# A graph layer's edge kernel: bias row, silu order, column counts and tail rearranged

## The chip, the cores and the metric

The kernel runs on one core of one Trainium2 chip. The metric is device time in microseconds (us) of one execution. TensorE is PE, VectorE DVE, ScalarE ACT, GpSimd POOL and SyncE SP. Each engine works off its own instruction stream in order; DMAs are issued by SP, ACT and POOL.

## The reference

12,500 nodes with 64 numbers each, 400,000 edges sorted by destination, 16 numbers per edge:

```python
m_in = jnp.concatenate([x[src], x[dst], edge_attr], axis=-1)
h = jax.nn.silu(m_in @ W1 + b1)
messages = jax.nn.silu(h @ W2 + b2)
agg = jax.ops.segment_sum(messages, dst, num_segments=x.shape[0])
out = layernorm(x + silu(concatenate([x, agg]) @ W3 + b3))
```

W1 is 144 x 64, W2 64 x 64, W3 128 x 64; all is float32.

## The kernel before, in words

128 edges are a tile, 3125 in all; 8 tiles are an octet (391), and three octets a chunk (131) whose dst and edge attributes are loaded together (`load`, L427 to L436: two `dr` DMAs and one `oh` DMA on SP). As the edges are sorted by dst, the destinations of an octet lie in a window of 48 nodes.

The first layer is a sum of three parts in PSUM (`first_layer`, L457). x[src] W1 comes ready from a table `pa` in HBM, gathered by POOL with one indirect DMA for each tile (`gather`, L396), and transposed by PE (L476). x[dst] W1 and the edge attributes come out of one product (L480): its weights `xw` hold the window's rows times W1 (`window_product`, L420, then `window_copy`, L425) and the attribute rows of W1, its data `oh` the one-hot of dst (`compare_dst`, L447) and the attributes. ACT applies silu with the bias `b1s` (L483). Two octets later PE does the second layer (`second_layer`, L492 and L494) and ACT its silu (L498); four octets later PE sums the messages by node with a second one-hot `eh` (L453; `add_up`, L507), and six later DVE adds the sums to `agg` (`add_window`, L512).

POOL is relieved in two ways. For some octets the first two tiles (a "pair") aren't gathered: ACT and DVE copy x[src] column by column, 64 partitions by 4 bytes, out of `xs`, a copy of x in SBUF, at addresses that they read into registers (`columns`, L294 to L303). ACOLS and VCOLS say how many columns each engine copies per octet and how they are cut into parts, LOADS how many addresses are read at once. PE multiplies the pair by W1 (`w1d`, L479). The indices of a pair come by a small DMA on SP (`index`, L374, tile `cxi`, three buffers), and DVE turns them into addresses (`address`, L382). For every 16th octet the second two tiles (`rx`) are fetched by SP, 16 rows of 256 bytes per octet (`rows`, L343 for the 16 addresses, L347 for the 16 DMAs).

The loop over octets (L626) writes out the order of PE, ACT, DVE and SP by hand; POOL's order is left to the framework. In one round o, SP issues the indices of pairs that begin in round o + 3, the chunk's load two octets ahead (L655), the window's x three octets ahead (`window_load`, L415, three buffers), and last the 16 rows. POOL gathers three octets ahead into five buffers. ACT: 32 columns, silu of octet o, 28 columns, silu of the second layer of octet o - 2. DVE: `agg`, `oh` of octet o + 1, 32 columns, `xw` and `eh` of octet o + 1, 32 columns.

When all edges of a group of 512 nodes (25 groups) are summed, its node layer is done between octets: `node_load`, `node_product` (L539 to L542, nine products), `node_silu` (L548), `node_stats`, and later, by batches of five groups, the root (L562), `divide` (L572) and `store` (L577). They are hung on rounds by `later`. The last two groups come after the loop, with a check of whether the windows held (L700 to L716); if not, a slow general form runs, which it doesn't here.

Of the kernel before, what the change touches and what calls it, by code (L numbers as in the profile page):

```python
# [20 lines left out]
P = 128  # L21
# [12 lines left out]
ACOLS = (32, 28)  # L34
VCOLS = (32, 32)
ROWS = 16
LOADS = (16, 8)
XBASE = (0, 64 << 18)
XADDR = 36864
# [61 lines left out]
def windows(ctx, tc, ident, badi, pa, x, xt, src_c, src_row, dst_c, dst_row, attr_t, dst_2, attr_2, base, w1, b1, w2, b2, w3, b3, out, edges):  # L101
# [33 lines left out]
    b1s = const.tile([P, 1], F32, name="b1s")  # L135
# [3 lines left out]
    for s in range(2):  # L139
        h = slice(s * D, (s + 1) * D)  # L140
        nc.scalar.dma_start(w1d[h, h], w1[0:D, :])
        nc.scalar.dma_start(b1s[h, :], b1.rearrange("(k o) -> k o", o=1))
# [93 lines left out]
    w1bb = fast.tile([D, 2, D], F32, name="w1bb")  # L236
    nc.vector.tensor_copy(w1bb, w1ab[:, 1:2, :].to_broadcast([D, 2, D]))
# [13 lines left out]
    with tc.tile_pool(name="gat", bufs=AHEAD + 2) as gat, tc.tile_pool(name="drp", bufs=2) as drp, \  # L251
# [3 lines left out]
            tc.tile_pool(name="msg", bufs=THIRD - SECOND + 1) as msg, tc.tile_pool(name="win", bufs=3) as win, \  # L255
# [3 lines left out]
            tc.tile_pool(name="cx", bufs=4) as cx, tc.tile_pool(name="cxi", bufs=3) as cxi, \  # L259
# [46 lines left out]

        def begun(o):

            first, behind = -(-(o - RAW) * RATE // (2 * P)), -(-(o + 1 - RAW) * RATE // (2 * P))
            return range(max(0, first), max(0, min(behind, len(pairs))))  # L310

        def index(o):
            for j in begun(o):
                t = cxi.tile([1, 2 * P], I32, name="cxi")
                e = octs[pairs[j]][1] * P
                nc.sync.dma_start(t, src_row[:, e:e + 2 * P])
                indices[j] = t

        def address(o):
            for j in begun(o):  # L320
                t = indices[j]
                for s in range(2):
                    h = slice(s * P, (s + 1) * P)
                    nc.vector.tensor_scalar(t[:, h], t[:, h], 4.0, float(XBASE[s] + XADDR), op0=OP.mult, op1=OP.add)

# [84 lines left out]
        def window_load(o):  # L410
            if o % 4 == 0:
                bases(ENG.SP, o)
            xr = win.tile([D, 2, S], F32, name="xr")
            frm = xt[:, ds(winreg.pop((ENG.SP, o)), S)]
            nc.sync.dma_start(xr, frm[:, None, :].to_broadcast([D, 2, S]))  # L415
            winrow[o] = xr
# [7 lines left out]
        def window_copy(o):  # L424
            nc.vector.tensor_tensor(xw[o % 3][:E, :], winrow.pop(o)[:E, :], mask[:E, :], op=OP.mult)  # L425
# [31 lines left out]
        def first_layer(o):  # L457
# [25 lines left out]
            nc.scalar.activation(h[:, :k], p1[:, :k], AF.Silu, bias=b1s)  # L483
# [48 lines left out]
        def node_product(q):  # L532
            c, n = groups[q]
            p = n // G
            assert p * G == n
            po = mis.tile([P, G, D], F32, name="mm")
            av = agg[:, c:c + n].rearrange("k (p i) -> k i p", i=G)
            xv = xs[0:D, c:c + n].rearrange("k (p i) -> k i p", i=G)
            nc.tensor.matmul(po[:p], ones[:, :p], b3r, start=True, stop=False, skip_group_check=True)  # L539
            for i in range(G):  # L540
                nc.tensor.matmul(po[:p, i, :], xv[:, i], w3x, start=False, stop=False, skip_group_check=True)  # L541
                nc.tensor.matmul(po[:p, i, :], av[:, i], w3s, start=False, stop=(i == G - 1), skip_group_check=True)  # L542
            nodes[q].append(po)
# [41 lines left out]
        todo = {}  # L585

        def later(o, f, *a):
            todo.setdefault(min(o, NO), []).append((f, a))
# [4 lines left out]
        for q in range(early):  # L593
            o = lead[due[q]] + LAST - 1 if q < rest else NO
            later(o - 1, node_load, q)
            later(o, node_product, q)
            later(o, node_silu, q)
            later(o + 2, node_stats, q)
        for q0, q1 in batches:
            o = lead[due[q1 - 1]] + LAST - 1  # L600
            later(o + 3, root, q0, q1)
            later(o + 4, inverse, q0, q1)
            for r in range(q1 - q0):
                later(o + 4 + 2 * r, divide, q0 + r)
                later(o + 5 + 2 * r, store, q0 + r)

# [16 lines left out]
        with tc.manual_schedule(engines={ENG.PE, ENG.Activation, ENG.DVE, ENG.SP}):  # L623
            compare_dst(0)
            compare_nodes(0)
            for o in range(NO + THIRD):  # L626
# [28 lines left out]
                if o + 2 < NO and octs[o + 2][3] and o + 2:  # L655
                    load(octs[o + 2][0])
# [38 lines left out]
                if o < NO:  # L695
                    for f, a in todo.get(o, []):
                        f(*a)


        evi = xs.bitcast(I32)[:, :3 * NCH]  # L700
        nc.gpsimd.iota(evi, pattern=[[STEP, NCH], [0, 3]], base=0, channel_multiplier=0)
        lag = xs[:, 3 * NCH:3 * NCH + NO]
        nc.vector.tensor_tensor(lag, evi[:, :NO], wb, op=OP.subtract)
        lim = nv.tile([P, 3], F32, name="lim")
        nc.vector.tensor_reduce(lim[:, 0:1], lims[:, 0, :], AX.X, OP.min)
        nc.vector.tensor_reduce(lim[:, 1:2], lims[:, 1, :], AX.X, OP.max)
        nc.vector.tensor_reduce(lim[:, 2:3], lag, AX.X, OP.max)
        bad = nv.tile([P, 3], F32, name="bad")
        nc.vector.tensor_scalar(bad[:, 0:1], lim[:, 0:1], 0.0, None, op0=OP.is_lt)
        nc.vector.tensor_scalar(bad[:, 1:2], lim[:, 1:2], float(S - 1), None, op0=OP.is_gt)  # L710
        nc.vector.tensor_scalar(bad[:, 2:3], lim[:, 2:3], float(LAG), None, op0=OP.is_gt)
        pc = mis.tile([1, 3], F32, name="mm")
        nc.tensor.matmul(pc, onec, bad, start=True, stop=True)
        bs = nv.tile([1, 1], F32, name="bs")
        nc.vector.tensor_reduce(bs, pc, AX.X, OP.add)
        nc.vector.tensor_copy(badi, bs)  # L716

        for o in range(NO + THIRD - LAST, NO):
            add_window(o)
        for f, a in todo.get(NO, []):  # L720
# [268 lines left out]
```

## Time and profile before

| | us |
|---|---|
| median of 3 runs (3440.99 to 3442.54) | 3441.17 |
| the profiled execution | 3453.06 |
| its span, first to last instruction | 3450.7 |
| POOL's last gather starts | 3399.90 |
| ACT's last first-layer silu starts | 3424.22 |
| mean granted TensorE clock | 0.68 |

The page of the profile gives busy time by engine and groups of instructions by line (L396 is line 396). A group's row reads: line, engine, operation, tile written <- tiles read, shapes, count | busy time, mean ns of one | idle time of the engine just before it, and who ended most of it. "issue" is idle time in which the engine waited for nothing that the profile shows. A source view lists one line's instructions with the least, median and longest duration and the first and last start. SPq, ACTq and POOLq are the engines' instruction sequencers.

### The profile page before, as it was taken

Reading aid. Unit: us, or ns where it says so; the run is one execution under the profiler, and the core shown is the slowest. Engines: PE = TensorE matmul, PEld = TensorE weight load, DVE = VectorE, ACT = ScalarE, POOL = GpSimd, SP = SyncE. Lnnn points to the kernel's source line nnn. Section 1 sums busy time; section 2 is a strip of 40 time slices with the busy share of each in tenths; the row PEclk is TensorE's granted clock in tenths of the full one; section 3 lists DMA queues with packets and bytes.
Section 4 is the critical chain, followed back from the end, with each engine's and each line's share of the span. In section 5 each row is a group of like instructions: output and inputs, shape, how many; then the busy total and the mean of one; then the engine's idle time right before and its main releaser. Section 6 shows DMA issues by size and latency. Waiting matters only on the chain. (4 is left out here: it accounts for less than half of the span.)

```text
span 3450.7 us, 104586 instructions
## 1 busy us (share of the span) xinstructions
PE 2554.8 (74%) x13750; PEld 1649.2 (48%) x13750; DVE 2517.4 (73%) x26396; ACT 2717.7 (79%) x23405; POOL 2569.0 (74%) x2724
## 2 busy tenths in 40 slices
PE   6877777777777677776777777777777677677777
PEld 4444544444445445444444445444445454444454
DVE  2477777777777777777777777777777777777775
ACT  2388788788887887888878888887788777878886
POOL 7777777777777777777777777777777777777773
PEclk9666667666667666776666666666666666766767
DMA  7423323323332332333332332333323323333322
GB/s 159 95 53 68 63 59 65 65 61 60 77 61 61 68 62 60 65 65 65 64 69 59 62 68 61 62 75 61 62 60 69 60 61 66 69 62 62 67 61 52
DMA packets 203931, 229.79 MB, mean 67 GB/s; under 512 B 133612, under 2 KB 141988, under 8 KB 202324
## 3 DMA queue, kind: packets, MB, share of 16 engines
q1 hardware_dynamic: 101528, 122.61, 16.1%
q0 software_dynamic: 86880, 89.14, 14.1%
q10 hardware_dynamic: 14812, 11.26, 1.4%
q14 instruction: 595, 4.87, 0.5%
q8 instruction: 116, 1.90, 0.2%
HBM read 216.36 MB, written 6.40 MB: 65 GB/s over the span
## 5 line engine op out<-in xcount | busy, mean ns | idle before, releaser
L396 POOL DMA_INDIRECT ga<-pa,sc x2619 | 2475.4, 945 | 802.2 <-issue 711.9
L303 ACT COPY cx<-xs 64x4 uint8 x22560 | 2216.5, 188 | 166.8 <-issue 122.0
L301 DVE TENSOR_REDUCE cx<-xs 64x4 uint8 x24032 | 1782.6, 150 | 544.7 <-issue 477.8
L507 PEld LDWEIGHTS pg<-eh,m 128*64 128x64 f32 x6250 | 301.0, 182 | 1046.8 <-issue 331.1
L507 PE MATMUL pg<-eh,m 128*64 128x48 f32 x6250 | 351.3, 271 | 580.9 <-DVE agg L512 523.0
L480 PE MATMUL p<-oh,xw 128*128 128x512 f32 (+1 forms) x758 | 601.0, 887 | 132.3 <-DVE xw L425 130.0
L494 PE MATMUL p<-w2d,h 128*128 128x128 f32 x3126 | 674.8, 383 | 0.0
L494 PEld LDWEIGHTS p<-w2d,h 128*128 128x128 f32 x3126 | 573.8, 275 | 133.1 <-issue 133.1
L498 ACT ACTIVATE m<-p 128x512 f32<-128x512 f32 x391 | 232.2, 594 | 255.5 <-PE p L494 249.0
L447 DVE TENSOR_TENSOR oh<-dr,wrow 96x512 f32<-96x512 int32 x391 | 264.4, 676 | 209.1 <-DMA dr<-in_dst 121.6
L483 ACT ACTIVATE h<-p,b1s 128x512 f32<-128x512 f32 x391 | 267.3, 684 | 139.2 <-PE p L480 86.1
L476 PE MATMUL p<-ident,ga 128*128 128x128 f32 x1310 | 336.9, 389 | 41.4 <-DMA ga<-pa,sc 41.4
L420 PE MATMUL mm<-w1bb,xr 64*96 64x128 f32 x782 | 252.9, 418 | 62.0 <-DMA xr<-in_xt 36.7
L476 PEld LDWEIGHTS p<-ident,ga 128*128 128x128 f32 x1310 | 199.6, 190 | 133.3 <-issue 110.3
L480 PEld LDWEIGHTS p<-oh,xw 128*128 128x128 f32 x758 | 176.7, 287 | 169.3 <-DVE xw L425 168.8
L453 DVE TENSOR_TENSOR eh<-wrow,dc 128x384 f32<-128x384 f32 x391 | 211.7, 541 | 0.0
L420 PEld LDWEIGHTS mm<-w1bb,xr 64*96 64x96 f32 x782 | 134.2, 224 | 140.2 <-issue 61.4
L492 PE MATMUL p<-b2r,one 3*128 3x512 bf16 x391 | 196.4, 502 | 0.0
L512 DVE TENSOR_TENSOR agg<-agg,pg 128x48 f32 x391 | 78.1, 200 | 74.2 <-PE pg L507 40.0
L479 PE MATMUL p<-cx,w1d 128*128 128x128 f32 x364 | 105.2, 387 | 22.7 <-ACT cx L303 22.7
L425 DVE TENSOR_TENSOR xw<-mm,mask 96x128 f32<-96x128 f32 x391 | 109.4, 280 | 13.4 <-PE mm L420 7.6
L396 POOL DMA_INDIRECT ga<-in_x,sc x96 | 91.5, 953 | 30.2 <-issue 27.7
(83 smaller groups left out, 767.6 us busy)
## 6 DMA issues: line engine op xcount, KB each, us to landing
rx<-pa SPq DMA_DIRECT2D x5888, 0.2 KB
dr<-in_dst SPq DMA_DIRECT2D x260, 288.0 KB
ga<-pa,sc POOLq DMA_INDIRECT x2619
oh<-in_attr SPq DMA_DIRECT2D x130, 192.0 KB
xr<-in_xt SPq DMA_DIRECT2D x391, 24.0 KB
xs<-in_xt ACTq DMA_DIRECT2D x12, 512.0 KB
pa<-v ACTq DMA_DIRECT2D x12, 256.0 KB
xa<-in_x SPq DMA_DIRECT2D x24, 128.0 KB
```

The costliest lines, as they stand in the source:

```text
L301: nc.vector.tensor_reduce(to, frm[:, :, None], AX.X, OP.max)
L303: nc.scalar.copy(to, frm)
L396: nc.gpsimd.indirect_dma_start(out=ga[:, i, :], out_offset=None, in_=x if o < RAW else pa[:, :], in_offset=bass.IndirectOffsetOnAxis(ap=sc ...
L420: nc.tensor.matmul(pw[:E, :], winrow[o].rearrange("k s w -> k (s w)"), w1bb.rearrange("k s m -> k (s m)"), start=True, stop=True)
L447: nc.vector.tensor_tensor(oh[:E, :], dr[:, e:e + w], wn[:E, o:o + 1].to_broadcast([E, w]), op=OP.is_equal)
L453: nc.vector.tensor_tensor(eh[:, :n], row[:, None, :].to_broadcast([P, n, S]), rel[:, t0:t0 + n, None].to_broadcast([P, n, S]), op=OP.is_equal)
L476: nc.tensor.matmul(p1[:, i, :], g2.rearrange("p s d -> p (s d)"), ident, is_transpose=True, start=(i == c), stop=False, skip_group_check=True)
L480: nc.tensor.matmul(p1[:, :k], xw[o % 3], oh, start=False, stop=True, skip_group_check=True)
L483: nc.scalar.activation(h[:, :k], p1[:, :k], AF.Silu, bias=b1s)
L494: nc.tensor.matmul(p2[:, 2 * i:2 * i + 2, :].rearrange("p s d -> p (s d)"), h[:, i, :], w2d, start=False, stop=(i == k - 1), skip_group_ch ...
L498: nc.scalar.activation(m[:, :n2], p2[:, :n2], AF.Silu)
L507: nc.tensor.matmul(pg[s * D:(s + 1) * D, :], m[:, i, :], eh[:, i, :], start=(i < 2), stop=(i >= n - 2), skip_group_check=True)
```

## The change

- b1 leaves the silu. The window product gets a 65th row: `w1bb` holds b1 there, and three fixed tiles `xr0` to `xr2` hold ones (they replace the pool `win`).
- `node_silu` of round o is done after the first-layer silu of round o + 1 (`behind`).
- A chunk's dst and attributes are loaded three octets ahead instead of two.
- ACT copies 40 + 32 columns per octet for 32 + 28; DVE copies 64 as before, in four parts of 16 around `xw` and `eh`. Addresses are read by 16. There are 196 pairs for 182; a pair is used one octet later, `cx` has five buffers for four, and pairs stop six octets from the end.
- XADDR, the address of `xs`, follows its new place.
- The end: the check `limits` and its product move into the last rounds (its iota on POOL stands ahead of the last 13 gathers), the last two groups load their x at round NO - 2, and their b3 and x products are done in round NO + 1, ahead of the last two sums.

```diff
-ACOLS = (32, 28)
-VCOLS = (32, 32)
+ACOLS = (40, 32)
+VCOLS = (16, 16, 16, 16)
-LOADS = (16, 8)
+LOADS = (16, 16)
-XADDR = 36864
+XADDR = 36832
+QUIET = 6
...
-    w1bb = fast.tile([D, 2, D], F32, name="w1bb")
-    nc.vector.tensor_copy(w1bb, w1ab[:, 1:2, :].to_broadcast([D, 2, D]))
+    w1bb = fast.tile([D + 1, 2, D], F32, name="w1bb")
+    nc.vector.tensor_copy(w1bb[:D], w1ab[:, 1:2, :].to_broadcast([D, 2, D]))
+    nc.sync.dma_start(w1bb[D:, :, :], b1.rearrange("(o s k) -> o s k", o=1, s=1).to_broadcast([1, 2, D]))
+    xrs = []
+    for k in range(3):
+        t = fast.tile([D + 1, 2, S], F32, name=f"xr{k}")
+        nc.vector.memset(t[D:], 1.0)
+        xrs.append(t)
...
-            o = RAW + -(-2 * P * (len(pairs) + 1) // RATE) + 1
-            if o >= len(octs) - 1:
+            o = RAW + -(-2 * P * (len(pairs) + 1) // RATE) + 2
+            if o >= len(octs) - QUIET:
...
-            nc.scalar.activation(h[:, :k], p1[:, :k], AF.Silu, bias=b1s)
+            nc.scalar.activation(h[:, :k], p1[:, :k], AF.Silu)
...
+            if q >= rest:
+                break
+            o = lead[due[q]] + LAST - 1
             later(o - 1, node_load, q)
             later(o, node_product, q)
-            later(o, node_silu, q)
+            behind.setdefault(o + 1, []).append(q)
...
-                if o + 2 < NO and octs[o + 2][3] and o + 2:
-                    load(octs[o + 2][0])
+                if o + 3 < NO and octs[o + 3][3]:
+                    load(octs[o + 3][0])
...
                 if o < NO:
                     first_layer(o)
+                for q in behind.get(o, []) if o < NO else []:
+                    node_silu(q)
...
                     window_copy(o + 1)
+                    columns(o, ENG.DVE, 1)
                     compare_nodes(o + 1)
-                columns(o, ENG.DVE, 1)
+                    columns(o, ENG.DVE, 2)
+                columns(o, ENG.DVE, 3)
...
+                if o == NO - 2:
+                    for q in range(rest, NG):
+                        node_load(q)
+                if o == NO - 1:
+                    bad = limits()
+                if o == NO + 1:
+                    verdict(bad)
+                    for q in range(rest, NG):
+                        node_product(q, 1)
...
-        for q in range(early, NG):
-            node_load(q)
-            node_product(q)
+        for q in range(rest, NG):
+            node_product(q, 2)
             node_silu(q)
             node_stats(q)
```

More of the change, by code (lines that the diff above doesn't have):

```diff
@@ L134, in windows @@
     nc.vector.memset(w1d, 0.0)
-    b1s = const.tile([P, 1], F32, name="b1s")
     w2d = const.tile([P, P], F32, name="w2d")
@@ L304, in columns @@
                 lo += n
[L307 to L324, printed above, removed]
         rpairs = []
@@ L530, in node_load, with node_product @@
             nodes[q] = [xa]
-        def node_product(q):
+        def node_product(q, part=0):
             c, n = groups[q]
@@ L535, in node_product @@
             assert p * G == n
[L536 removed]
+            if part < 2:
+                nodes[q].append(mis.tile([P, G, D], F32, name="mm"))
+            po = nodes[q][1]
             av = agg[:, c:c + n].rearrange("k (p i) -> k i p", i=G)
             xv = xs[0:D, c:c + n].rearrange("k (p i) -> k i p", i=G)
[L539 removed]
+            if part < 2:
+                nc.tensor.matmul(po[:p], ones[:, :p], b3r, start=True, stop=False, skip_group_check=True)
             for i in range(G):
[L541 to L543 removed]
+                if part < 2:
+                    nc.tensor.matmul(po[:p, i, :], xv[:, i], w3x, start=False, stop=False, skip_group_check=True)
+                if part != 1:
+                    nc.tensor.matmul(po[:p, i, :], av[:, i], w3s, start=False, stop=(i == G - 1),
+                                     skip_group_check=True)
         def node_silu(q):
@@ L697, in windows @@
                         f(*a)
[L700 to L716, printed above, removed]
+                if o == NO - 2:
[7 more added lines that the diff above has]
+                        node_product(q, 1)
         for o in range(NO + THIRD - LAST, NO):
             add_window(o)
+        for q in behind.get(NO, []):
+            node_silu(q)
         for f, a in todo.get(NO, []):
             f(*a)
-        for q in range(early, NG):
-            node_load(q)
-            node_product(q)
+        for q in range(rest, NG):
+            node_product(q, 2)
             node_silu(q)
```

32 lines of the change are left out of this document (25 added, 7 removed).

## The prediction

> **What bounds the kernel now.** I read the page first, for the busy shares and for the groups with their idle time.
>
> ```profile
> PE 2554.8 (74%) x13750; PEld 1649.2 (48%) x13750; DVE 2517.4 (73%) x26396; ACT 2717.7 (79%) x23405; POOL 2569.0 (74%) x2724
> ...
> L396 POOL DMA_INDIRECT ga<-pa,sc x2619 | 2475.4, 945 | 802.2 <-issue 711.9
> L303 ACT COPY cx<-xs 64x4 uint8 x22560 | 2216.5, 188 | 166.8 <-issue 122.0
> L301 DVE TENSOR_REDUCE cx<-xs 64x4 uint8 x24032 | 1782.6, 150 | 544.7 <-issue 477.8
> ...
> L498 ACT ACTIVATE m<-p 128x512 f32<-128x512 f32 x391 | 232.2, 594 | 255.5 <-PE p L494 249.0
> ...
> L483 ACT ACTIVATE h<-p,b1s 128x512 f32<-128x512 f32 x391 | 267.3, 684 | 139.2 <-PE p L480 86.1
> ```
>
> No engine is over 79% busy, and ACT and DVE wait. POOL looks like the bound: a gather takes 945 ns and is followed by idle time that nothing but issue explains, (2475.4 + 802.2) / 2619 = 1.252 us each. But the page leaves SP out, since issuing DMAs doesn't count as busy. So the second view is SP's lines by source, from 290 to 3355 us, with the line of the first silu (ACT) and of the gathers (POOL) over the same stretch.
>
> ```profile
> L415 SPq EVENT_SEMAPHORE  x352: 17/17/17, 290.4 to 3347.8; - x176
> ```
> ```profile
> L483 ACT ACTIVATE h<-p,b1s x352: 673/687/693, 293.4 to 3350.1; 128x512 f32<-128x512 f32 x176
> ```
> ```profile
> L396 POOL DMA_INDIRECT ga<-pa,sc x2451: 940/944/1457, 290.0 to 3354.9; - x189
> ```
>
> SP goes round once per octet: (3347.8 - 290.4) / 351 = 8.710 us. ACT keeps (3350.1 - 293.4) / 351 = 8.709 us, the same pace. SP's 352 waits ahead of the window load lasted 17 ns each, so SP found its condition true every time: it follows nobody. SP's timeline shows what fills the 8.7 us.
>
> ```profile
> 2432.08 0.65 SPq L415 DMA_DIRECT2D xr<-in_xt  x1
> 2434.32 6.11 SPq L347 DMA_DIRECT2D rx<-pa  x16
> 2440.53 0.23 SPq L374 DMA_DIRECT2D cxi<-in_src_row  x1
> 2440.99 0.61 SPq L415 DMA_DIRECT2D xr<-in_xt  x1
> 2443.19 5.11 SPq L347 DMA_DIRECT2D rx<-pa  x16
> ```
> ```profile
> 2457.17 0.24 SPq L374 DMA_DIRECT2D cxi<-in_src_row  x1
> 2457.51 0.80 SPq L435 DMA_DIRECT2D dr<-in_dst  x2
> ```
>
> The 16 single row copies take 5.1 to 6.1 us; the 2.2 us between a window load and the first row are the load's issue and the reading of 16 addresses; the rest is the indices and the dst load. Where does the consumer hang on SP? At the rows, each 16 octets, and at the dst load, each three.
>
> ```profile
> L347 SPq DMA_DIRECT2D rx<-pa x32: 224/225/281, 3341.2 to 3355.7; - x32
> ```
> ```profile
> L476 PE MATMUL p<-ident,rx x1: 448/448/448, 3357.8 to 3357.8; 128*128 128x128 f32 x1
> ```
> ```profile
> DVE oh L447 <- DMA dr<-in_dst: 121.6, 71, 5.6
> ```
> ```profile
> ACT z L548 <- PE mm L542: 123.2, 24, 7.2
> ```
>
> The last row is issued at 3355.7 and the transposition that reads it starts 2.1 us later (octet 381). **SP's instruction stream is the bound from about 290 to 3356 us.** POOL is close: an octet's 8 gathers are fewer by two for 124/256 of a pair and by two for 16/256 of a set of rows, 6.91, times 1.252 = 8.65 us.
>
> A rule speaks against this reading. The Trainium skill, DMA: Bandwidth & Descriptors, section "Issuing engines are not separate DMA queues", says that the sequencer's time to start a DMA is usually small beside the DMA. By it SP would be free and POOL would set the pace; that is the last case below. Here the trace disagrees: copies of 256 bytes, 16 in 5.1 to 6.1 us, fill most of an octet.
>
> **The change part by part.**
>
> *b1 by a 65th row.* h loses its pointer operand: 684 to about the 594 ns of m, same shape, 0.09 x 391 = 35 us of ACT's time, beside SP's stream and so worth nothing by itself. The window product has 65 partitions where it had 64; the node products show both widths.
>
> ```profile
> L542 PE MATMUL mm<-w3s,agg 128*128 128x64 f32 (+1 forms) x200 | 71.1, 455 | 0.0
> L541 PE MATMUL mm<-w3x,xs 64*128 64x64 f32 (+1 forms) x200 | 70.6, 452 | 0.0
> ```
>
> 128 partitions take 455 ns and 64 take 452: 0.
>
> *Silu of nodes an octet later.* The 123.2 us of ACT waiting (24 times 5.1 us) go. ACT is late after each such stop but SP isn't held, except through the index tile, whose buffer SP may refill only when ACT has read it.
>
> ```profile
> 274.81 0.38 ACT L548 ACTIVATE z<-mm 128x256 f32<-128x256 f32 x1 [3.60 <-PE mm L542]
> ```
> ```profile
> L374 SPq EVENT_SEMAPHORE  x12: 17/28/7543, 153.5 to 275.0; - x12
> L374 SPq DMA_DIRECT2D cxi<-in_src_row x8: 231/234/240, 131.4 to 281.0; - x8
> ```
> ```profile
> SPq L374 <- ACTq L294: 8.1, 15, 1.8
> ```
>
> At 275.0 SP stops, until 281.0, and runs free from there. Without ACT's stop of 3.6 us its reading would come some 4 us earlier: -4 us for SP's whole course (bounds 0, and -13 if the stop of 7.5 us at 153.5 goes too). From 290 us on the same wait totals 8.1 us; its long ones fall two octets behind a silu of nodes: -6 (bounds -8, and +12 if the closer pairs make it wait more). New wait: PE's window product two octets later needs the node product's bank back; ACT has an octet for it, I take 0.
>
> *dst an octet earlier.* SP issues the same DMAs, so its pace stays. The 121.6 us of DVE's waiting go; late next are the rows, which hold the same lag: 0 (bounds -8, one rows' lag less, and 0). The attr DMA now waits for the first layer of the octet before; behind it stand the window load and 16 rows. SP's window load of a round comes some 6 us behind that round's silu (3347.8 + 8.71 against 3350.1), so 0. Where SP overtook, each of 130 chunks would cost.
>
> *72 and 64 columns.* 196 pairs for 182: 28 gathers fewer, 35 us of POOL, off the path. 14 more index loads on SP: 2457.17 to 2457.51 is 0.34 us for one, +5 us. ACT gets 12 columns more per octet. Its pass with no wait in it is in these rows:
>
> ```profile
> 3395.42 0.69 ACT L483 ACTIVATE h<-p,b1s 128x512 f32<-128x512 f32 x1
> 3396.00 2.75 ACT L303 COPY cx<-xs 64x4 uint8 x28
> 3398.66 0.59 ACT L498 ACTIVATE m<-p 128x512 f32<-128x512 f32 x1
> 3399.14 3.13 ACT L303 COPY cx<-xs 64x4 uint8 x32
> 3402.18 0.68 ACT L483 ACTIVATE h<-p,b1s 128x512 f32<-128x512 f32 x1
> ```
>
> 6.76 us; 12 columns at 3.13/32 = 0.098 add 1.17, the bias takes 0.09 away: 7.84. Address loads of 16 where there were 8 were never in the middle of a run here: between 0 (hidden by queued copies) and about 1 us each, two per octet. A load of 16 takes some 1.0 us and 8 copies 0.8, so I take 0.2 each: 8.25 us, under SP's 8.71. DVE keeps its 64 columns, with four loads for six; 6.44 us busy and 1.2 us of issue per octet stay below SP. At either end of its bounds, 0.
>
> *Pairs stop early, tail rearranged.* From octet 381 SP's rows are over. POOL may be five octets ahead, the number of gather buffers, so octet 386's gathers start when octet 381 is transposed. Rows of the end now:
>
> ```profile
> 3399.90 0.94 POOL L396 DMA_INDIRECT ga<-pa,sc  x1 [0.30 <-issue]
> ```
> ```profile
> 3424.22 0.58 ACT L483 ACTIVATE h<-p,b1s 128x384 f32<-128x384 f32 x1 [0.38 <-PE p L480]
> ```
> ```profile
> L701 POOL IOTA xs<- x1: 1213/1213/1213, 3419.8 to 3419.8; 128x393 int32 x1
> ```
>
> Now ACT's last silu follows the last gather by 23 us, since columns run on to octet 387. After, octets 386 to 390 are gathered whole: 37 x 1.252 = 46.3, plus the iota that now stands 13 gathers from POOL's end, 1.2 + 0.3. From the transposition at 3357.8: 0.9 for the rest of it, 47.8 of POOL, and from gather to silu about 5 us (an estimate: it is 23 now, with landing, transposition and product inside): 53.7 us, where it is 66.4. That is -13 (bounds -17 and -4, the latter if the columns weren't what held ACT). Behind that the x part of the last two node products, 2 x 70.6/25 = 5.6 us, now stands between the last second layer and the last two sums: what it saves behind the sums it costs ahead of them, 0 (bounds -3 and +3). PE's clock decides a little more:
>
> ```profile
> 3404.74 2.08 PE L494 MATMUL p<-w2d,h 128*128 128x128 f32 x8
> ```
> ```profile
> 3426.98 1.16 PE L494 MATMUL p<-w2d,h 128*128 128x128 f32 x8
> ```
>
> The same product takes 2.08 or 1.16 us. The end runs at the fast one today; I take 0 (bounds 0 and +4). The Trainium skill, TensorE: Matmul & The Clock Gate, section "What's actually happening", says that an idle window of about 3.4 us halves the clock. By it the gathers' pace of 10 us per octet would bring the slow one, and the sum would be some 3 us longer.
>
> *The rest*: the offset of xs (the program has the same instructions per column), buffers, a DMA less on ACT's queue at the start: 0.
>
> **Sum** against the execution's own time: -4 - 6 + 5 - 13 = -18 us on 3453.1 us (the span and 2.4 us around it). The median of the runs is 3441.2, 11.9 us lower; I take 18 off that: **3423 us**, 0.5% faster. At their ends the terms give -13 - 8 - 8 + 5 - 17 - 3 = -44 and 0 + 12 + 5 - 4 + 3 + 4 = +20.
>
> **The rivals.**
> *The tail gives, SP takes back* (0.18). Pairs come every 1.88 octets for 2.06, and the index buffers stay three, so SP waits for ACT more often. Ten to 25 us of such waits, where 8.1 are now, bring 3433 to 3448: 3440. Against it: the waits follow node silus, which leave.
> *ACT becomes the bound* (0.16), the slower side. Today ACT loses to PE (249.0 + 86.1)/391 = 0.86 us per octet, and 122.0/376 = 0.32 to address loads behind a stop. If both stay, an octet takes 7.84 + 1.18 = 9.02 us, and 350 octets x 0.31 = 109 us, less 18: 3532. It decides from 8.71 - 7.84 = 0.87 us of stalls per octet; with 1.0 it is 8.84, 46 us, less 18: 3469. Against it: 6.76 us without a wait happens, and what ACT waits for today is PE, which waits for DVE, which waits for dst.
> *SP isn't the limit* (0.08): it only runs as fast as it is let, and POOL sets the pace. Then the last gather ends 35 us earlier with the iota's 1.5 added, 3400.8 - 33.5 = 3367.3, the last silu follows 5 us behind and the tail of 3450.7 - 3424.2 = 26.5: 3398.8 of span, 52 us off: 3389. The 17 ns speak against it.
>
> **How the numbers follow.** The forecast case has 0.58. About 0.2% (7 us) is what a measurement of this kernel can tell from no change. Faster: 0.58 + 0.08 = 0.66; same: 0.17; slower: 0.17. The range is 3405 to 3454: it leaves out the POOL case below and most of the ACT case above, and of the terms' ends, 3397 and 3461, the corners where all meet.
>
> **What would show it.** SP's window loads still 8.7 us apart with waits of 17 ns; ACT's silu at that pace, its waiting for nodes and DVE's for dst gone; gathers stopping for transposed buffers from mid-run on; the last silu 3 to 8 us behind the last gather. Wrong would be: ACT's copies end to end with a pace over 8.75 us, SP's index waits in tens of us, or a pace near 8.5.

## The result and the profile after

| | before | after |
|---|---|---|
| median of 20 runs, us | 3440.59 (3432.20 to 3452.27) | 3424.48 (3416.92 to 3437.32) |
| ratio, 95% interval | | 0.9958 (0.9948 to 0.9968) |
| profiled execution, us | 3453.06 | 3420.95 |
| its span, us | 3450.7 | 3418.8 |
| POOL's last gather starts, us | 3399.90 | 3385.79 |
| ACT's last first-layer silu starts, us | 3424.22 | 3390.22 |
| mean granted TensorE clock | 0.68 | 0.697 |

The medians lie 16.1 us apart; by the interval of the ratio the change makes the kernel between 11 and 18 us faster. 3423 us was forecast, with 3405 to 3454 as the range. The two profiled executions lie 32 us apart, because that of before is 12.5 us over its median (slower than all 20 timed ones) and that of after 3.5 us under it; a reading of the two profiles has to tell these 16 us of chance from the rest. Of the seven chips on which the experiments ran, three take 5164 to 5256 us for the kernel before, so each experiment is read only against the kernel before on its own chip.

The page of after, in the columns of the page of before:

```profile
PE 2283.9 (67%) x13764; PEld 1545.4 (45%) x13764; DVE 2433.6 (71%) x26003; ACT 3109.1 (91%) x27413; POOL 2542.7 (74%) x2696
...
L382 POOL DMA_INDIRECT ga<-pa,sc x2591 | 2449.8, 945 | 813.4 <-issue 702.5
L308 ACT COPY cx<-xs 64x4 uint8 x26568 | 2646.4, 187 | 60.7 <-issue 37.2
...
L406 PE MATMUL mm<-w1bb,xr 65*96 65x128 f32 x782 | 234.6, 395 | 839.2 <-DMA xr<-in_xt 673.6
...
L469 ACT ACTIVATE h<-p 128x512 f32<-128x512 f32 x391 | 231.7, 592 | 144.8 <-PE p L466 99.9
...
L484 ACT ACTIVATE m<-p 128x512 f32<-128x512 f32 x391 | 231.4, 592 | 43.5 <-PE p L480 31.2
```

ACT is busy for 91% of the span, where it was 79%, and yet waits less: the second silu (L484) waited 255.5 us and waits 43.5. h takes 592 ns for 684, just as m. POOL issues 28 gathers fewer. The new large number stands at PE's window product: it waits 839.2 us, 673.6 of them for the window load `xr`, which SP issues. The same row of before, with all that ended its waits:

```profile
L420 PE MATMUL mm<-w1bb,xr 64*96 64x128 f32 x782 | 252.9, 418 | 62.0 <-DMA xr<-in_xt 36.7 <-DMA ga<-pa,sc 14.4 <-ACT z L548 10.9
```

SP's waits ahead of the window load of after from 290 to 3355 us by source, its last row copies, the transposition that reads them, and the first silu over the 342 octets from octet 40 to 381:

```profile
L401 SPq EVENT_SEMAPHORE  x240: 17/17/28, 295.4 to 3351.6; - x120
```
```profile
L333 SPq DMA_DIRECT2D rx<-pa x12: 227/228/237, 3330.1 to 3334.1; - x12
```
```profile
L462 PE MATMUL p<-ident,rx x1: 448/448/448, 3335.7 to 3335.7; 128*128 128x128 f32 x1
```
```profile
L469 ACT ACTIVATE h<-p x342: 582/597/599, 382.6 to 3339.6; 128x512 f32<-128x512 f32 x171
```

The same silu of before, over the same octets:

```profile
L483 ACT ACTIVATE h<-p,b1s x342: 673/687/693, 389.3 to 3362.2; 128x512 f32<-128x512 f32 x171
```

Ahead of the window load SP still never waits (17 ns, 28 at most, in the 240 rounds that have such a row), and the loads themselves, 358 in this stretch, take 615 ns at the median and 1432 at most. The silus give the pace: after (3339.6 - 382.6) / 341 = 8.672 us, before (3362.2 - 389.3) / 341 = 8.718 us. Octet 40 comes 6.7 us earlier. Whether the 0.046 us per octet, 16 us in all, belong to the change can be told only from other executions with the middle part of before. The experiments below have two, each on its own chip: 8.677 us (e8_tail_full) and (3348.2 - 390.9) / 341 = 8.672 us (e5_tail_again). So they look like chance of the profiled execution of before, and not like the change.

The end of after on the timeline (start, duration, engine, line, operation, idle time ahead of it):

```profile
3369.39 1.23 POOL L602 IOTA xs<- 128x393 int32 x1
...
3384.37 0.60 ACT L469 ACTIVATE h<-p 128x512 f32<-128x512 f32 x1 [8.17 <-PE p L466]
...
3385.79 1.06 POOL L382 DMA_INDIRECT ga<-pa,sc  x1 [0.30 <-issue]
...
3390.22 0.49 ACT L469 ACTIVATE h<-p 128x384 f32<-128x384 f32 x1 [1.68 <-PE p L466]
```

The last silu now follows the last gather by 4.4 us, where it followed by 24.3. The end is POOL's: ACT's silu of octet 389 waits 8.17 us for gathers.

### The profile page after: what moved, and what is told of

It is laid out like the page before. It is cut to its first block, busy times and chain, and to the rows that moved or that the text cites. A ratio compares the mean times of both kernels' runs of the same rounds, so it can differ in the third digit from the quotient of the medians.

```text
span 3418.8 us, 107012 instructions
## 1 busy us (share of the span) xinstructions
PE 2283.9 (67%) x13764; PEld 1545.4 (45%) x13764; DVE 2433.6 (71%) x26003; ACT 3109.1 (91%) x27413; POOL 2542.7 (74%) x2696
## 3 DMA queue, kind: packets, MB, share of 16 engines
q1 hardware_dynamic: 101560, 122.63, 16.1%
## 5 line engine op out<-in xcount | busy, mean ns | idle before, releaser
L382 POOL DMA_INDIRECT ga<-pa,sc x2591 | 2449.8, 945 | 813.4 <-issue 702.5
L308 ACT COPY cx<-xs 64x4 uint8 x26568 | 2646.4, 187 | 60.7 <-issue 37.2
L306 DVE TENSOR_REDUCE cx<-xs 64x4 uint8 x23608 | 1684.2, 153 | 527.3 <-issue 477.2
L406 PE MATMUL mm<-w1bb,xr 65*96 65x128 f32 x782 | 234.6, 395 | 839.2 <-DMA xr<-in_xt 673.6
L480 PE MATMUL p<-w2d,h 128*128 128x128 f32 x3126 | 571.7, 339 | 0.0
L406 PEld LDWEIGHTS mm<-w1bb,xr 65*96 65x96 f32 x782 | 141.0, 226 | 890.3 <-DMA xr<-in_xt 785.1
L480 PEld LDWEIGHTS p<-w2d,h 128*128 128x128 f32 x3126 | 483.1, 236 | 114.7 <-issue 114.7
L493 PE MATMUL pg<-eh,m 128*64 128x48 f32 x6250 | 334.8, 263 | 104.8 <-DVE agg L498 101.8
L433 DVE TENSOR_TENSOR oh<-dr,wrow 96x512 f32<-96x512 int32 x391 | 263.6, 674 | 150.4 <-DMA dr<-in_dst 70.8
L469 ACT ACTIVATE h<-p 128x512 f32<-128x512 f32 x391 | 231.7, 592 | 144.8 <-PE p L466 99.9
L462 PEld LDWEIGHTS p<-ident,ga 128*128 128x128 f32 x1296 | 236.1, 196 | 84.6 <-issue 80.3
L484 ACT ACTIVATE m<-p 128x512 f32<-128x512 f32 x391 | 231.4, 592 | 43.5 <-PE p L480 31.2
L498 DVE TENSOR_TENSOR agg<-agg,pg 128x48 f32 x391 | 78.2, 200 | 188.3 <-PE mm L533 113.3
L478 PE MATMUL p<-b2r,one 3*128 3x512 bf16 x391 | 177.5, 454 | 0.0
```

Of the source, the lines that this page charges most:

```text
L306: nc.vector.tensor_reduce(to, frm[:, :, None], AX.X, OP.max)
L308: nc.scalar.copy(to, frm)
L382: nc.gpsimd.indirect_dma_start(out=ga[:, i, :], out_offset=None, in_=x if o < RAW else pa[:, :], in_offset=bass.IndirectOffsetOnAxis(ap=sc ...
L406: nc.tensor.matmul(pw[:E, :], winrow[o].rearrange("k s w -> k (s w)"), w1bb.rearrange("k s m -> k (s m)"), start=True, stop=True)
L433: nc.vector.tensor_tensor(oh[:E, :], dr[:, e:e + w], wn[:E, o:o + 1].to_broadcast([E, w]), op=OP.is_equal)
L462: nc.tensor.matmul(p1[:, i, :], g2.rearrange("p s d -> p (s d)"), ident, is_transpose=True, start=(i == c), stop=False, skip_group_check=True)
```

## The experiments

**Only the early stop of the pairs** (e1_tail and e5_tail_again), in the kernel before:

```diff
-            if o >= len(octs) - 1:
+            if o >= len(octs) - 6:
                 break
             pairs.append(o)
```

> The kernel before, in which only the pairs stop 6 octets ahead of the end (176 pairs' last ones fall away; the rest of the end stays as it was). My theory: SP's instruction stream sets the pace up to octet 381 and the columns of ACT and DVE hold the end, so the end alone gives about -13 us against the kernel before (between -17 and -4), and SP's window loads stay 8.7 us apart. Rival: the gain of the whole change (-16 us by the medians) was made along the way by SP, and the end gives under 4 us: then 0 to -4 us here.

> The kernel before, in which only the pairs stop 6 octets ahead of the end, once more, since in the run of this edit before this one the kernel before itself took 5164 us and not 3441. If it takes about 3441 us here, my theory gives -13 us for this edit (between -17 and -4), and the rival, that the end gives nothing, 0 to -4 us. If it takes about 5164 us again, instruction issue of ACT and DVE is the bound there (1460 us of ACT's time ahead of its copies is put down to issue, 122 us in the profile of 3451 us), and the edit gives 0 to -10 us.

On a chip where the kernel before takes 5164.36 us: 5157.18, ratio 0.999 (0.9971 to 1.001). On one where it takes 3443.05 us: 3445.22, ratio 1.0007 (0.9998 to 1.0016). So nothing of the -13 us comes. The timeline of the second run's end says why:

```profile
3386.87 1.23 POOL L701 IOTA xs<- 128x393 int32 x1
3388.14 0.57 DVE L703 TENSOR_TENSOR xs<-xs,wb 128x391 f32<-128x391 int32 x1 [33.64 <-POOL xs L701]
...
3390.24 1.09 PE L507 MATMUL pg<-eh,m 128*64 128x48 f32 x16 [29.63 <-DVE agg L512]
```

The check behind the loop isn't part of the order written by hand. With the pairs gone from the last octets, its first DVE instruction (L703) was placed ahead of the last six octets' compares in DVE's stream, while the iota that it reads stands behind most of the last gathers in POOL's. DVE stopped for 33.64 us and PE behind it for 29.63. The run says nothing of the early stop by itself. It does show what the move of `limits` into the loop is needed for.

**dst three octets ahead, alone** (e2_dst), in the kernel before:

```diff
-                if o + 2 < NO and octs[o + 2][3] and o + 2:
-                    load(octs[o + 2][0])
+                if o + 3 < NO and octs[o + 3][3]:
+                    load(octs[o + 3][0])
```

> The kernel before, in which only the loads of dst and attributes are started three octets ahead, not two. My theory: SP issues the same instructions and never waits, so its pace of 8.7 us stays and the time is the same, 0 us (down to -8 for one lag less at the end). Rival: it is the wait of DVE for dst, 121.6 us in 71 pieces, that holds the consumer, and the consumer holds SP: then -15 to -30 us.

**The early nodes' silu an octet later, alone** (e3_nodes), in the kernel before:

```diff
-            later(o, node_silu, q)
+            if q < rest:
+                behind.setdefault(o + 1, []).append(q)
+            else:
+                later(o, node_silu, q)
...
                     first_layer(o)
+                for q in behind.get(o, []) if o < NO else []:
+                    node_silu(q)
```

> The kernel before, in which only the silu of the early nodes comes an octet later in ACT's order (their product stays where it was; the last group of nodes is as before). My theory: ACT's 24 stops of 5.1 us go, and through them some of SP's waits for index buffers: -10 us (-4 at the start, -6 later), between 0 and -19. Rival: ACT's stops are made up for behind SP's pace and SP's waits stay: 0 us; or PE's window product waits for the bank that the node product holds longer: above 0.

Both ran beside a kernel before of 5164.36 us: 5142.90 (0.9965, 0.9947 to 0.9983) and 5144.50 (0.9969, 0.9949 to 0.9989). By the ratios that is 18 and 16 us off, each give or take some 10 us. What was expected was worked out for another bound: on that chip an octet takes some 13.2 us (5164.36 / 391), and the rows of the groups show what fills it. From e1_tail, same chip:

```profile
L396 POOL DMA_INDIRECT ga<-pa,sc x2625 | 2478.3, 944 | 2483.5 <-PE p L476 1394.4
L303 ACT COPY cx<-xs 64x4 uint8 x22200 | 2358.4, 188 | 1495.8 <-issue 1460.5
L301 DVE TENSOR_REDUCE cx<-xs 64x4 uint8 x23624 | 1861.6, 150 | 1584.4 <-issue 1521.5
```

A gather takes 944 ns and a copy 188, as everywhere, but ACT loses 1460.5 us ahead of its copies to "issue", where it lost 122.0. What the two edits are worth at 3441 us stays open.

**b1 back in the silu** (e4_bias), in the changed kernel:

```diff
-            nc.scalar.activation(h[:, :k], p1[:, :k], AF.Silu)
+            nc.scalar.activation(h[:, :k], p1[:, :k], AF.Silu, bias=b1s)
```

with the window product at 64 rows again and XADDR at its old place.

> The changed kernel with b1 back in the silu's pointer operand and the window product of 64 rows. My theory: ACT isn't the bound, so its 0.09 us more per octet lie beside SP's stream: as the changed kernel, -16 us against the kernel before (between -20 and -10). Rival: ACT, which is 91% busy now, sets the pace: 391 x 0.09 = 35 us more, which is +19 us against the kernel before.

On the same chip 5467.39 us, ratio 1.0592 (1.057 to 1.0614). That is 303 us more, far from the 35 us of a bias. It has the changed kernel's 72 columns on ACT, 4008 copies more than before (26568 for 22560), on a chip where ACT's copies are issued late; with 60 columns the kernel is faster than before on another such chip (e9_cols60, below). For the chip of the forecast this run doesn't decide between the theories.

**The whole end, alone** (e6_tail_full and e8_tail_full): the early stop, `limits` and `verdict` in the loop, and the last node products in two parts, in the kernel before.

> The kernel before with the whole end of the change: the pairs stop 6 octets ahead of the end, the check of the bounds (iota and what follows it) is issued in the last octets at a fixed place, and the x part of the last node products stands ahead of the last sums. In the run with the early stop alone DVE waited 33.6 us for the iota, which stood behind the gathers in POOL's order while DVE's order had its reader ahead of the last six octets. My theory: with the reader at its place that wait goes, and the end gives the -13 us of the prediction (between -17 and -4) against the kernel before; from the last row copy to the end of the span it takes about 85 us, as in the changed kernel (84.7), where it is 95.0 in the kernel before. Rival: POOL's last gathers set the end in any case, 37 and an iota for 29, and it takes 95 us or more: 0 us.

> The kernel before with the whole end of the change, once more, since the last run of it was on a chip on which the kernel before takes 5254 us. Where the kernel before takes about 3441 us: my theory -13 us (between -17 and -4) and about 85 us from the last row copy to the end of the span, where it is 95.0 before; rival 0 us and 95 us or more, since POOL's last gathers set the end. Where it takes over 5000 us: about -10 us, as in the run before this one.

Beside 5253.60 us: 5239.47, ratio 0.9979 (0.9965 to 0.9992). Beside 3442.38 us: 3437.48, ratio 0.9989 (0.9980 to 0.9998), that is 4.9 us off. DVE's stop is gone, and still most of the 13 us isn't there. From the last row copy (3340.7 us) to the end of the span it takes 95.1 us, as the rival said; it is 95.0 in the profile of before and 84.7 in that of after. The second run's silus over the 342 octets, then the transposition of octet 381, the gathers from there on, and the end:

```profile
L483 ACT ACTIVATE h<-p,b1s x342: 673/687/692, 389.4 to 3348.2; 128x512 f32<-128x512 f32 x171
```
```profile
L476 PE MATMUL p<-ident,rx x1: 445/445/445, 3342.1 to 3342.1; 128*128 128x128 f32 x1
```
```profile
L396 POOL DMA_INDIRECT ga<-pa,sc x51: 940/944/1020, 3341.2 to 3404.8; - x51
```
```profile
3404.76 1.02 POOL L396 DMA_INDIRECT ga<-pa,sc  x1 [0.30 <-issue]
...
3409.16 0.58 ACT L483 ACTIVATE h<-p,b1s 128x384 f32<-128x384 f32 x1 [1.69 <-PE p L480]
```

The last silu follows the last gather by 4.4 us, as in the changed kernel: ACT's columns no longer hold the end. But it comes 67.1 us after the transposition, where the changed kernel takes 54.5 (3390.2 - 3335.7). The same view of the changed kernel, from its transposition on:

```profile
L382 POOL DMA_INDIRECT ga<-pa,sc x40: 940/944/1057, 3336.0 to 3385.8; - x40
```

40 gathers are left there, 51 here. POOL isn't five octets ahead. Its middle part is that of before and runs at (3348.2 - 389.4) / 341 = 8.677 us per octet. POOL needs 8.65 us for an octet's gathers: it gains 0.03 us per octet and doesn't reach its limit by octet 381. The rival, that POOL's gathers set the end in any case, holds in this run.

**ACT's columns back at 60** (e9_cols60 and e12_cols60), in the changed kernel:

```diff
-ACOLS = (40, 32)
+ACOLS = (32, 28)
```

> The changed kernel with ACT's columns back at 60 per octet (pairs of columns as many as before, less the early stop: 34 more gathers, 2721). New theory: POOL gathers without a gap from 2.8 us on in the kernel before, so the number of gathers x 1.252 us is a floor of its own beside SP's stream: 2721 x 1.252 + 2.8 = 3409 us to the last gather's end, and 33 us behind it (4.4 to the last silu, 28.6 to the end): 3442 us of span, so 0 to +4 us against the kernel before, all of the gain gone. Theory of the prediction: POOL is off the path and the 12 columns cost SP 5 us of index loads: 3419 us, -21 us. On a chip where the kernel before takes over 5000 us, issue on ACT decides, and 4400 copies fewer bring it near the kernel before: within 1%.

> The changed kernel with ACT's columns back at 60 per octet, once more, for a chip on which the kernel before takes about 3441 us: 34 gathers more than the changed kernel, 2721. New theory: POOL's gathers are a floor beside SP's stream, since POOL has no gap from its first gather to its last in the kernel before; in the run of the whole end alone 2721 gathers ended at 3406 us, so 3406 + 33 (4.4 to the last silu and 28.6 to the end, as in the changed kernel) = 3439 us of span, -3 to +3 us against the kernel before, and POOL without a gap: the gain of the end hangs on the columns. Theory of the prediction: POOL is off the path, and 12 columns fewer spare SP 5 us of index loads: -21 us. Where the kernel before takes over 5000 us: -1%, as in the run of this edit before.

Beside 5256.09 us: 5195.10, ratio 0.9879 (0.9852 to 0.9905). Beside 3442.97 us: 3448.86, ratio 1.0021 (1.0010 to 1.0031), 5.9 us slower than before. The theory of the prediction gave -21 us for it; it falls. The new one gave -3 to +3 and misses by 3 us; for the first chip it gave less than 1%, and the run is 1.2% faster. All of the gain hangs on the twelve columns: with them -16.1, without +5.9, each against the kernel before on its own chip, so they are worth some 22 us on top of the other parts. The gathers of the second run, and what PE waited for:

```profile
L382 POOL DMA_INDIRECT ga<-pa,sc x2625: 943/947/1353, 123.5 to 3411.3; - x188
```
```profile
PE p L462 <- DMA ga<-pa,sc: 411.3, 283, 5.8
PE mm L406 <- DMA xr<-in_xt: 377.6, 154, 13.8
```

(3411.3 - 123.5) / 2624 = 1.253 us from one gather to the next: POOL has no gap, and PE waits for it 283 times. In this kernel POOL is a bound, and the one that sets the end. The 342 silus of this run and its gathers from the transposition of octet 381 on (3332.6 us):

```profile
L469 ACT ACTIVATE h<-p x342: 582/597/599, 385.5 to 3339.3; 128x512 f32<-128x512 f32 x171
```
```profile
L382 POOL DMA_INDIRECT ga<-pa,sc x63: 943/947/1129, 3332.3 to 3411.3; - x63
```

The pace in the middle is (3339.3 - 385.5) / 341 = 8.662 us, as with the columns. But 63 gathers are left behind the transposition where the changed kernel has 40, and from octet 381's silu to the end of the span it takes 3447.6 - 3339.3 = 108.3 us, where the changed kernel takes 79.2. So what the columns are worth stands at the end. The gathers of the kernel before:

```profile
L396 POOL DMA_INDIRECT ga<-pa,sc x2619: 940/944/1457, 123.5 to 3399.9; - x188
```

(3399.9 - 123.5) / 2618 = 1.251 us: POOL has next to no gap in the kernel before either. The changed kernel:

```profile
L382 POOL DMA_INDIRECT ga<-pa,sc x2591: 938/944/1603, 122.8 to 3385.8; - x200
```

(3385.8 - 122.8) / 2590 = 1.260 us, so there POOL does stop, for some 8 ns x 2590 = 21 us in all. This fits the 22 us: 34 gathers fewer take 34 x 1.253 = 43 us off POOL, and some 21 of them come back as POOL's stops. The 5.9 us aren't resolved. The gathers of e12_cols60 take 947 ns at the median and not 944, which over 2721 is 8 us, and 36.3 us follow the start of the last one, where 33.0 do in the changed kernel. Whether the 3 ns are the chip's or the kernel's isn't shown, since the kernel before wasn't profiled on that chip; if they are the chip's, its time there has them too.

**The attributes on ACT's queue** (e7_attr_act), in the changed kernel:

```diff
-            nc.sync.dma_start(oh[E:, e], attr_2[:, d])
+            nc.scalar.dma_start(oh[E:, e], attr_2[:, d])
```

> The changed kernel, in which the attribute load of each three octets is issued by ACT, not by SP. My theory: SP's instruction stream is the bound, and an attribute issue is 0.42 us of it per three octets, 0.14 per octet, so the pace falls from 8.65 us to POOL's 6.81 x 1.252 = 8.53 us or a little above: 350 x 0.12 = -42 us more than the changed kernel, some -58 us against the kernel before (between -35 and -60). Rival: ACT, 91% busy, sets the pace now and an issue on it takes 0.4 us: +0.13 us per octet, 46 us, which is +30 us against the kernel before. Second rival: PE's wait for the window's columns is the landing of that load and not SP's lateness: -16 us, as the changed kernel.

Beside 5253.60 us: 5666.38, ratio 1.0798 (1.0779 to 1.0818). The changed kernel itself wasn't timed on this chip, and with its 72 columns e4_bias was 5.9% slower on another such chip, so what the moved load costs isn't shown; for the other chips the run decides nothing.

**Half the row copies, 72 columns on DVE** (e10_rows8_dve72 and e11_rows8_dve72), in the changed kernel:

```diff
-VCOLS = (16, 16, 16, 16)
-ROWS = 16
+VCOLS = (16, 16, 16, 24)
+ROWS = 8
```

> The changed kernel with 8 row copies per octet on SP for 16, and 72 columns on DVE for 64, so that POOL issues the same 2687 gathers. Theory: SP's stream (some 2.75 us per octet shorter) is what holds the changed kernel at 8.66 us; then POOL goes without a gap, 2687 x 1.252 + 2.8 = 3367 us to the end of the last gather, and 33 us more: 3400 us of span, -38 us against the kernel before (between -30 and -42). Rival: ACT, 91% busy, or DVE sets the pace in the changed kernel: then no better than it, -16 us, and if it is DVE, which gets 8 columns more, 0.6 us per octet slower. On a chip where the kernel before takes over 5000 us: +5%, as other forms of the changed kernel there.

> The changed kernel with 8 row copies per octet on SP for 16 and 72 columns on DVE for 64, once more, for a chip on which the kernel before takes about 3441 us. There SP's stream is some 2.75 us per octet shorter and POOL issues the same 2687 gathers as the changed kernel. Theory: SP holds the changed kernel at 8.66 us; POOL then goes without a gap, 2687 x 1.252 + 2.8 = 3367 us to the end of the last gather and 33 us more: -38 us against the kernel before (between -30 and -42). Rival: ACT, 91% busy, or DVE sets the pace of the changed kernel: -16 us at best, and slower than the changed kernel where DVE's 8 columns more are what counts. Where the kernel before takes over 5000 us: +1%, as in the run before.

Beside 5256.09 us: 5321.25, ratio 1.0109 (1.0081 to 1.0137). Beside 3447.25 us: 3472.43, ratio 1.0069 (1.0055 to 1.0083), 25 us slower, where SP as the only bound promised 38 us faster. The second run's silus, what SP waited for, and what PE waited for:

```profile
L469 ACT ACTIVATE h<-p x342: 581/597/598, 385.0 to 3391.7; 128x512 f32<-128x512 f32 x171
```
```profile
SPq L360 <- ACTq L299: 1124.9, 198, 16.3
```
```profile
PE pg L493 <- DVE agg L498: 777.3, 294, 6.6
PE mm L406 <- DMA xr<-in_xt: 75.0, 36, 12.8
```

SP is free here: it waits 1124.9 us for ACT to give index buffers back, and PE's wait for `xr` is down from 673.6 to 75.0 us, while its wait for `agg` is up from 101.8 to 777.3. The pace is nevertheless (3391.7 - 385.0) / 341 = 8.817 us, 0.145 slower. The engines by windows, first of the changed kernel, then of this one (length; PE, PEld, DVE, ACT and POOL busy; granted clock, share and GB/s of DMA):

```profile
1000.00:2000.00 1000.00, 649.21 (x3990) 443.20 (x3990) 738.56 (x8058) 957.03 (x8561) 755.54 (x801) 0.70 0.31 64
2000.00:3000.00 1000.00, 659.35 (x4017) 444.87 (x4015) 745.35 (x8110) 960.40 (x8577) 746.12 (x789) 0.70 0.31 64
```
```profile
1000.00:2000.00 1000.00, 693.36 (x3947) 493.77 (x3946) 797.87 (x8869) 943.19 (x8446) 737.18 (x781) 0.68 0.31 63
```

Per octet of the stretch from 1000 us ACT is busy 0.95703 x 8.672 = 8.30 us there and 0.94319 x 8.817 = 8.32 here; DVE 6.40 and 7.03. ACT has the same work and more waiting; what grew is DVE, and PE's new wait is for DVE's `agg`. The rows point to a loop of DVE, PE and ACT right behind SP, which 8 columns more on DVE put at 8.82 us. Where it stands with DVE's 64 columns and a free SP wasn't tried, so that SP alone holds the changed kernel at 8.67 isn't shown.

## Why the prediction came out

The number was right, 3423 for 3424, and the sums by stretches of time were near: -4 was given for the start, -1 for the middle (-6 and +5) and -13 for the end. Measured in the profile of after against that of e8_tail_full, whose start and middle are those of before, octet 40 comes 389.4 - 382.6 = 6.8 us earlier, the middle is 341 x (8.677 - 8.672) = 1.7 us shorter, and from octet 381's silu to the end of the span it takes 3418.8 - 3339.6 = 79.2 us, where the profile of before takes 3450.7 - 3362.2 = 88.5, so 9.3 us less: -17.8 in all for -16.1 by the medians. The start gave more than forecast and the end less, so that the sum came out is partly luck. What was wrong is which edit earns it.

- **What bounds the kernel.** "SP's instruction stream is the bound" was too simple. SP waits for nobody at its window loads in either kernel, and PE now waits 673.6 us for its window loads. But POOL hardly waits in the kernel before either: its gathers come 1.251 us apart to the last. The prediction took from the page that POOL is "close" at 8.65 us and left it off the path. Two streams that both run without a gap, at 8.65 and some 8.67 us, are two bounds; the second to end decides, and that is where POOL comes in.
- **72 and 64 columns: the step that failed.** "28 gathers fewer, 35 us of POOL, off the path" and +5 us for index loads. The columns are worth -22 us (e12_cols60 against the result). In the middle they do nothing, as said: 8.672 us with them, 8.662 without. They let POOL come nearly five octets ahead by octet 381, and the formula for the end, 37 gathers behind octet 381's transposition, takes just that for granted: 40 were left with the columns, 63 without them in e12_cols60 and 51 in e8_tail_full. The condition stood in the text ("POOL may be five octets ahead"); what fulfils it was booked as a cost.
- **The end.** -13 was for the early stop and what goes with it. Alone it gives -4.9 us by the medians, and by the profiles hardly any of it at the end (3435.8 - 3348.2 = 87.6 us from octet 381's silu, for 88.5); with the columns the end gives 9.3. From the transposition to the last silu 53.7 us were worked out and 54.5 measured, for 66.4. Behind the last silu 28.6 us are measured for 26.5: the 0 there was 2 us too good. The products that were moved stand where PE is needed, ahead of the last two sums, from 3396.35 to 3401.15 us, and PE's clock falls there: the 16 products of a sum take 0.67 us at 3394.50 and 1.09 at 3401.08, as in these rows of after.

```profile
3394.50 0.67 PE L493 MATMUL pg<-eh,m 128*64 128x48 f32 x16
...
3396.35 0.69 PE L528 MATMUL mm<-b3r,ones 1*128 1x256 f32 x2
...
3400.05 1.10 PE L531 MATMUL mm<-w3x,xs 64*53 64x64 f32 x8
...
3401.08 1.09 PE L493 MATMUL pg<-eh,m 128*64 128x48 f32 x16
```

  The granted clock is 1.00 from 3391.2 to 3397.9 us and 0.50 from 3398 to 3418; in the kernel before it was 1.00 up to 3435, with both last sums done by 3431.7. So the term for PE's clock, taken as 0 with +4 at its end, has a share in the 2 us; how much is the clock and how much the products' place isn't shown.
- **The start and the index waits.** ACT's stops for nodes fell from 123.2 us in 24 to 9.9 in 2, and SP's index waits from 290 us on from 8.1 us to 6.2. -4 and -6 were given. The start brought 6.7, the later waits next to nothing. SP's stop at 275 us, from which the -4 was read, is 1.1 us long for 6.0; the earlier one, 7.5 us at 153.5, didn't go but is 15.8 us long at 143.7. The waiting for node products didn't vanish either: DVE's addition to `agg` (L498) waits 113.3 us in 22 pieces for them, where it waited 11.1 in 8. The silu's new place and the early dst weren't measured alone where 3441 us is the time.
- **dst early.** DVE's wait fell from 121.6 us in 71 to 70.8 in 28, not to nothing, and the pace stayed, as said. "Late next are the rows" was wrong: late next is the window load, 673.6 us of PE's waiting; the rows are 85.8.
- **b1 and ACT.** 594 ns were given and 592 measured. 8.25 us were given for ACT's pass of an octet; two passes without a wait, from silu to silu, take (2447.25 - 2430.47) / 2 = 8.39 in these rows of after.

```profile
2430.47 0.58 ACT L469 ACTIVATE h<-p 128x512 f32<-128x512 f32 x1
...
2438.87 0.60 ACT L469 ACTIVATE h<-p 128x512 f32<-128x512 f32 x1
...
2447.25 0.59 ACT L469 ACTIVATE h<-p 128x512 f32<-128x512 f32 x1
```

  That b1's move is worth nothing alone isn't tested where 3441 us is the time. The 65 rows cost nothing to be seen: 395 ns, where 64 rows took 418 at a slightly lower clock.
- **The rivals.** "SP takes back" is out: its index waits didn't grow. "ACT becomes the bound" didn't come: the pace is 8.67 us. But a pass of 8.39 leaves only 0.28 us per octet. "POOL sets the pace" got 0.08 and holds half: in the kernel with 60 columns POOL sets the end, and in the changed one it stops for some 21 us, so that its 3389 us weren't reached.
- **The two rules.** The Trainium skill, DMA: Bandwidth & Descriptors, section "Issuing engines are not separate DMA queues", calls the time to start a DMA small. In the changed kernel PE waits 673.6 us for loads that stand in this stream of starts, so the trace still disagrees. The Trainium skill, TensorE: Matmul & The Clock Gate, section "What's actually happening", has the clock halved after an idle window of about 3.4 us and full after about 3.4 us of sustained work. Half clock did come at the pace of the gathers, but the rows of this end don't show such windows. The 8.17 us ahead of the silu are ACT's wait; PE's own gaps there are 2.2 us at most, since it transposes each tile as it lands, and yet the second layer's product takes 2.08 us. The clock of 0.50 from 3398 us on follows 6.7 us, from 3391.2 to 3397.9, in which PE was busy throughout. So what sets the clock here stays open.

```profile
3382.11 0.45 PE L462 MATMUL p<-ident,ga 128*128 128x128 f32 x1 [2.02 <-DMA ga<-pa,sc]
...
3385.76 2.08 PE L480 MATMUL p<-w2d,h 128*128 128x128 f32 x8
...
3391.40 1.16 PE L480 MATMUL p<-w2d,h 128*128 128x128 f32 x8
```
```profile
3391.20:3397.90 6.70, 6.70 (x65) 5.26 (x65) 0.89 (x5) 1.69 (x3) 0.00 (x0) 1.00 0.01 2
3398.00:3418.00 20.00, 8.19 (x57) 6.55 (x56) 5.21 (x30) 2.35 (x4) 0.00 (x0) 0.50 0.05 15
```

The columns of the last two rows are those of the windows above; the third number from the end is the granted clock.

The signs that were to show it came, apart from the dst wait's remainder: window loads without waits, the silu at that pace, gathers that stop for transposed buffers in the second half (POOL has 801 instructions between 1000 and 2000 us and 789 in the next 1000), and the last silu 4.4 us behind the last gather. They show the sum, not the shares of the edits: only single edits did that.

## What to carry to other kernels

An engine that works without a gap from its first instruction to its last can set the end, even where nobody waits for it in the middle: count its instructions, multiply by their spacing, and compare with the end of the span before calling its work off the path. A term for the end of a kernel rests on how far ahead the feeding engine is there, so ask which edit puts it there, and try the term alone. Code behind a hand-written order can be placed inside it, so an edit that frees its inputs can move it ahead of the work that counts.

## What the runs showed of the hardware

- Three of seven chips took 5164 to 5256 us for the kernel that takes 3442 to 3447 us on the other four. Gathers (944 ns) and copies (188 ns) are as long there; what grows is idle time put down to issue, 1460.5 for 122.0 us ahead of ACT's copies and 1521.5 for 477.8 us ahead of DVE's. The packets of the DMA instruction queue took no longer as far as the page's shares tell, which have one digit: 0.3% of 16 engines in 5164.5 us (248 us) for 0.5% in 3450.7 us (276 us). The cause stays open. Kernels with 72 columns on ACT and 16 rows on SP, each with one more edit, are 5.9% and 8.0% slower than the kernel before there, that with 60 columns 1.2% faster, so the sign of this change may well be the other one on such a chip; the changed kernel itself wasn't run on one.
- The kernel before repeats within 20 us in 20 executions (3432.20 to 3452.27), and its pace per octet differs as much between profiles (8.718 us and, with the same middle part in e8_tail_full and e5_tail_again, 8.677 and 8.672), so one profile of each kernel can't tell a change of 0.04 us per octet.
- Indirect gathers of 128 x 64 came 1.251 to 1.253 us apart over some 3280 us with next to no gap, 944 ns at the median in the kernel before and 947 in e12_cols60.
- The granted TensorE clock fell from 1.00 to 0.50 at about 3398 us in the changed kernel, right behind 6.7 us in which PE was busy throughout; the same 16 products took 0.67 us ahead of it and 1.09 behind it.
